# Layer 3's causal mask moves from TensorE to VectorE, with other orders of the attentions' first products

## The chip, the cores and the metric

The kernel runs on one core of a Trainium2 chip. The metric is the device time of one execution in microseconds, the median of several runs. A core has five engines with queues of their own: PE (TensorE, matrix products into PSUM), DVE (VectorE), ACT (ScalarE), POOL (GpSimd) and SP (SyncE). PEld is PE's weight load, which overlaps its products. PSUM has eight banks of 512 fp32 columns; a tile that is computed there holds its banks until its readers are done.

## The reference

The program is a chain of four layers on an input of shape (8, 512, 128), each with half a feed-forward block, a mixer and another half block. The change concerns the mixers of layers 1 and 3, both attentions with 16 heads of 8 dimensions over 512 positions; layer 3's is causal:

```python
def _L3_attn_ref(embeddings, Wq, bq, Wk, bk, Wv, bv, Wo, bo):
    ...
    scores = jnp.einsum('bhqk,bhsk->bhqs', q, k) / jnp.sqrt(jnp.float32(dk))
    causal_mask = jnp.triu(jnp.ones((s, s), dtype=bool), k=1)
    scores = jnp.where(causal_mask, jnp.float32(-1000000000.0), scores)
    weights = jax.nn.softmax(scores, axis=-1)
    ctx = jnp.einsum('bhqs,bhsk->bhqk', weights, v)
    concat = ctx.transpose(0, 2, 1, 3).reshape(b, s, d)
    return concat @ Wo + bo
```

Layer 1's is the same without the mask, with another residual and a normalisation behind it.

## The kernel before

An attention handles one of eight batches after another. The 16 heads are four groups `g` of four heads (`j` or `h`), each head in a band of 32 partitions; the 512 positions are four chunks `c` of 128. The softmax needs each query's largest score before the exponential, with queries on partitions, but the exponentials themselves are made with keys on partitions, so the scores are computed twice:

- The *first products* (`maxima`, PSUM tile `first`, three buffers): for each chunk of queries, head and group, one product of `qT` with `kT`, and a read on DVE (L1673) that puts minus the row maximum into `max`. In layer 3 chunk c needs only its first 128 (c + 1) keys. There the diagonal block is masked on PE: a product of a bf16 identity with a bf16 mask tile (0 or -1e30) is added into the same PSUM columns behind the first product. Chunks 1 and 0 are narrow, so two groups' products of chunk 1 (2 x 256 columns) and four groups' products of chunk 0 (4 x 128) share one bank and one read. That makes 64 first products and 44 reads a batch in layer 3, 64 and 64 in layer 1. `firsts` lists their order. When a group's 16 maxima are there, POOL makes `copies`; `maxima_turned` turns all of them by PE into `mT`.
- The *weighted sums* (`weighted`): a step for each group and chunk of keys, in two halves of two heads. A half makes two score products (`pair`, a tile of two banks, two buffers), adds minus the maxima by two more products (`mT`, `max_rows`), and ACT takes the exponential into `e` (L1781). In layer 3 chunk c of keys has only the 512 - 128 c queries from its own on, and POOL clears the upper triangle (L1783). At the end of a second half, `product` multiplies the `e` of the step *before* with `v` and adds into `av`; after the last step of a pair of groups ACT copies `av` to `ctx`.

The first products of batch b + 1 run beside the weighted sums of batch b: each half-step takes two of them from the list. In layer 1 both stand between the half's score products and its max_rows products; in layer 3 both stand behind the max_rows products. Their reads are issued behind the exponential, and a mask product with its read.

PE's order is the order of emission (`in_order`). The other work of a batch (projections of batch b + 2, spreading of q and k over the bands by `spread_out`, the turning of maxima, the end of batch b - 1) is cut into pieces, and `_SLOTS` says behind which of the 32 half-steps each piece stands. `lead` is how many first products of batch 1 run before the first half-step. `fill` is a list by chunk: so many products of a bf16 tile of zeros with one of ones, 512 columns, are added into `av` behind the sums with v of that chunk, which changes no value; layer 3 has (0, 2, 0, 1), layer 1 none.

The 64 first products of batch 0 of layer 3, with their reads, are pieces of `attention_head`; they run among the end of the experts, in tiles that are called `mm` there.

All products go through one helper, so their line is L329 and they are told apart by tiles: `pair<-qkT` scores, `first<-qkT` first products, `first<-mask,ident_bf` masks, `pair<-mT,max_rows` maxima, `av<-e,v` sums, `av<-ones,zeros` fills, `pair<-lead,spread` and `pair<-trail,spread` spreads. L1595 makes the second half of q and k in two parts, and L1338 is a running sum of layer 2.

Of the kernel before, what the change touches and what calls it, by code (L numbers as in the profile page):

```python
# [26 lines left out]
P = 128  # L27
# [175 lines left out]
def _attention_pack(p, wq, bq, wk, bk, wv, bv, wo, bo):  # L203
# [30 lines left out]
        lead=4, attended=(6, 9, 10), spread=(2, 3), turned=30,  # L234
        projected=(3, 5, 5, 7, 12, 18, 19), spread0=(20, 24), fill=(0, 2, 0, 1),
# [56 lines left out]
class _Kernel:  # L292
# [1138 lines left out]
    def attention_constants(self, ctx):  # L1431
# [8 lines left out]
        self.mask = keep.tile([P, 4, P], BF16, name="mask")  # L1440
        self.ident_bf = keep.tile([P, P], BF16, name="ident_bf")
# [25 lines left out]
        nc.vector.tensor_copy(self.mask, self.wide(self.w["const", "mask_qk"]))  # L1467
        nc.vector.tensor_copy(self.ident_bf, self.ident)
# [3 lines left out]
    def attention(self, key, causal):  # L1472
# [9 lines left out]
        with ExitStack() as s:  # L1482
# [6 lines left out]
            for g in range(2 if causal else 1):  # L1489
                self.spread_out(1, g)  # L1490
# [51 lines left out]
    def between(self, b):  # L1542
# [10 lines left out]
        if b + 1 < NB:  # L1553
            late = (2, 3) if self.causal else (1, 2, 3)
            put(at["spread"], [lambda g=g: self.spread_out(b + 1, g) for g in late])
            put([at["turned"]], [lambda: self.maxima_turned(b + 1)])
        if b + 2 < NB:
            put(at["projected"], self.projections(b + 2))
            early = (0, 1) if self.causal else (0,)
            put(at["spread0"], [lambda g=g: self.spread_out(b + 2, g) for g in early])  # L1560
# [82 lines left out]
    def maxima(self, b):  # L1643
# [7 lines left out]
        def product(c, j, gs, k, bank):  # L1651

# [3 lines left out]
            if k == 0:  # L1656
                name, bufs = self.banks["first"]
                bank.append(self.ps.tile([P, L], F32, name=name, bufs=bufs))
            sc = bank[0][:, : len(gs) * n].rearrange("p (g n) -> p g n", n=n)
            self.mm(  # L1660
                sc[:, k, :],
                q["qT"][gs[k]][r, bass.ts(c, P)],
                q["kT"][gs[k]][r, :n],
                start=k == 0,
                stop=not causal,
            )
            if k + 1 < len(gs):
                return None

            def read():  # L1670
                if causal:
                    self.mm(sc[:, :, n - P :], self.ident_bf, self.mask[:, : len(gs), :], start=False)
                nc.vector.tensor_reduce(  # L1673
                    mx[:, c, j, gs[0] : gs[-1] + 1], sc, AX.X, ALU.max, negate=True
                )
# [241 lines left out]
```

## Time and profile before

| what | us |
|---|---|
| median of 3 runs | 2370.53 |
| lowest and highest run | 2366.5, 2375.26 |
| span of the profiled execution | 2372.5 |
| layer 1's attention, about | 803 to 1251 |
| one batch of it | 54.0 |
| layer 3's attention, about | 1900 to 2300 |
| one batch of it | 51.6 |

The profile is one execution. A line of a group gives the kernel's line, engine, operation, output and input tiles and shapes, the count, then busy time and mean length of one, then the idle time of the engine just before such instructions and what ended it. A chain of waits is followed back from the last instruction to what released each one. Products on PE are pipelined, so the length of one holds its latency; the distance from start to start says what it takes of PE. Layer 3's batch holds on PE 32 mask products of 128 columns, 8 of 256 and 4 of 512:

```profile
L329 PE MATMUL first<-mask,ident_bf 128*128 128x128 bf16 x32 | 4.6, 224 | 0.0
L329 PE MATMUL av<-ones,zeros 128*128 128x512 bf16 x12 | 4.0, 384 | 0.0
L329 PE MATMUL first<-mask,ident_bf 128*128 128x256 bf16 x8 | 2.3, 283 | 0.0
L329 PE MATMUL first<-mask,ident_bf 128*128 128x512 bf16 x4 | 1.6, 389 | 0.0
```

### The profile page before, as it was taken

The page shows a single profiled execution, that of the slowest core. Times are in us where ns is not written, and L with a number is a line of the kernel's source. Part 1 is how long each engine was busy: PE and PEld are TensorE (multiplying, and loading weights), DVE is VectorE, ACT ScalarE, POOL GpSimd, SP SyncE. Part 2 cuts the span into 40 slices and gives each one's busy share as a digit, 9 for nine tenths or more (in the row PEclk, how much of TensorE's full clock was granted, in tenths as well). Part 3 has the DMA queues.
Part 4 walks back from the last instruction along what each step waited for, and adds up shares of the span by engine and source line. Part 5 has one row for each costly group of instructions (what it writes and reads, how often), then busy time and mean ns, then how long its engine had stood idle before and what let it go on. Part 6 is the DMA issues. An engine that isn't in the chain of part 4 may idle for free.

```text
span 2372.5 us, 30011 instructions
## 1 busy us (share of the span) xinstructions
PE 2109.1 (89%) x10967; PEld 1001.9 (42%) x10967; DVE 1631.6 (69%) x3830; ACT 1269.6 (54%) x1857; POOL 660.6 (28%) x923
## 2 busy tenths in 40 slices
PE   7679999979998888999996999896789999999989
PEld 3344444444433333333332444444445444444444
DVE  4556775368888788888827889888776556666611
ACT  3545665323322376777772446666674355555554
POOL 1124433013212011111113233446552123333330
PEclk9778998979999999999997999998897999999999
DMA  3000000000000000000000000000000000000001
GB/s 124 1 1 1 1 1 1 14 10 1 1 1 1 1 1 1 1 1 1 1 1 7 1 1 1 0 1 1 0 1 0 1 1 1 1 1 1 2 1 36
DMA packets 10035, 13.07 MB, mean 6 GB/s; under 512 B 416, under 2 KB 8736, under 8 KB 9760
## 3 DMA queue, kind: packets, MB, share of 16 engines
q1 hardware_dynamic: 7776, 10.11, 1.3%
q8 instruction: 86, 1.41, 0.3%
q10 hardware_dynamic: 2112, 1.05, 0.2%
q14 instruction: 61, 0.50, 0.1%
HBM read 9.06 MB, written 2.10 MB: 5 GB/s over the span
## 4 chain that ended last, share of the span: by engine, by line
PE 60%; DVE 23%; POOL 7%; ACT 7%; issue 3%; DMA 0%; ACTq 0%; DVEq 0%; SPq 0%; POOLq 0%
PE pair L329 11%; PE av L329 8%; PE mm L329 8%; PE po L329 6%; PE pu L329 5%; PE first L329 4%; DVE max L1673 4%; PE pg L329 3%; ACT e L1781 3%; PE ck L329 2%; PE pr L329 2%; DVE act L942 2%; PE big L329 1%; PE ph L329 1%; DVE xn L355 1%
## 5 line engine op out<-in xcount | busy, mean ns | idle before, releaser
L1673 DVE TENSOR_REDUCE max<-first 128x1 f32<-128x512 f32 (+3 forms) x756 | 468.3, 664 | 173.4 <-PE first L329 166.1
L1781 ACT ACTIVATE e<-pair 128x1024 f32<-128x1024 f32 (+3 forms) x512 | 436.5, 864 | 239.3 <-PE pair L329 227.1
L329 PE MATMUL first<-qkT 32*128 32x512 f32 (+3 forms) x896 | 267.9, 443 | 30.5 <-DVE max L1673 28.7
L329 PE MATMUL pair<-qkT 32*128 32x512 f32 (+3 forms) x1024 | 222.5, 454 | 20.0 <-ACT e L1781 14.6
L329 PE MATMUL av<-e,v 128*32 128x512 f32 (+3 forms) x2048 | 238.9, 536 | 0.1
L941 ACT ACTIVATE act<-pg 128x512 f32<-128x512 f32 x144 | 85.6, 596 | 212.9 <-PE po L329 122.0
L329 PEld LDWEIGHTS pair<-qkT 32*128 32x128 f32 x1024 | 95.2, 185 | 233.6 <-ACT e L1781 133.2
L329 PE MATMUL pair<-mT,max_rows 32*128 32x512 f32 (+3 forms) x1024 | 190.4, 374 | 1.7 <-DVE mT L1715 1.7
L329 PE MATMUL pu<-xT,w_moe 128*128 128x512 f32 x288 | 158.4, 632 | 18.8 <-DVE act L942 14.0
L1783 POOL TENSOR_SCALAR_AFFINE_SELECT e<-e 128x256 f32<-128x256 f32 x256 | 103.4, 407 | 253.4 <-ACT e L1781 253.1
L329 PE MATMUL po<-act,w_moe 128*128 128x512 f32 x288 | 161.3, 647 | 5.4 <-DVE act L949 4.2
L329 PE MATMUL pg<-xT,w_moe 128*128 128x512 f32 x288 | 150.5, 620 | 4.4 <-ACT act L941 3.3
L329 PEld LDWEIGHTS first<-qkT 32*128 32x128 f32 x896 | 119.6, 185 | 69.4 <-DVE max L1673 66.9
L942 DVE TENSOR_TENSOR act<-act,pu 128x512 f32<-128x512 f32 x144 | 97.8, 679 | 28.8 <-PE pu L329 23.5
L1679 POOL COPY copies<-max 128x128 f32<-128x128 f32 x64 | 23.6, 424 | 272.4 <-DVE max L1673 272.4
L329 PEld LDWEIGHTS pair<-mT,max_rows 32*128 32x128 f32 x1024 | 96.9, 188 | 3.0 <-DVE mT L1715 2.7
L1673 DVE TENSOR_REDUCE max<-mm 128x1 f32<-128x512 f32 (+3 forms) x108 | 70.9, 665 | 36.7 <-PE mm L329 35.5
L949 DVE TENSOR_TENSOR act<-act,big 128x512 f32<-128x512 f32 x128 | 86.3, 677 | 12.3 <-PE big L329 11.8
L329 PEld LDWEIGHTS pu<-xT,w_moe 128*128 128x128 f32 x288 | 50.2, 196 | 76.8 <-DVE act L942 37.0
L329 PEld LDWEIGHTS po<-act,w_moe 128*128 128x128 f32 x288 | 50.5, 199 | 63.5 <-issue 28.1
L978 POOL TENSOR_TENSOR ge<-ge,w_moe 128x64 f32<-128x64 f32 (+1 forms) x32 | 42.8, 1336 | 119.1 <-DVE ge L976 113.6
L329 PEld LDWEIGHTS pg<-xT,w_moe 128*128 128x128 f32 x288 | 51.1, 195 | 57.2 <-issue 40.1
(423 smaller groups left out, 4398.2 us busy)
## 6 DMA issues: line engine op xcount, KB each, us to landing
w_moe<-in_moe SPq DMA_DIRECT2D x1, 2392.0 KB, 14.0
out<-x SPq DMA_DIRECT2D x8, 256.0 KB, 2.3
x<-in_u ACTq DMA_DIRECT2D x4, 256.0 KB, 6.6
x<-in_u SPq DMA_DIRECT2D x4, 256.0 KB, 6.4
w_mixer<-in_l0a SPq DMA_DIRECT2D x1, 960.5 KB, 8.2
w_mixer<-in_l1a SPq DMA_DIRECT2D x1, 769.0 KB, 4.8
w_ffn<-in_l0f SPq DMA_DIRECT2D x1, 578.0 KB, 7.2
w_ffn<-in_l2f SPq DMA_DIRECT2D x1, 560.0 KB, 3.3
```

The lines of the kernel that those rows point to most:

```text
L329: self.nc.tensor.matmul(out, lhsT, rhs, start=start, stop=stop)
L355: nc.vector.tensor_scalar(xn[:, c, :], x[:, c, :], mv[:, c, 0:1], rstd[:, c : c + 1], ALU.subtract, ALU.mult)
L941: nc.scalar.activation(act, pg, AF.Silu)
L942: nc.vector.tensor_tensor(act, act, pu, ALU.mult)
L949: nc.vector.tensor_tensor(act, act, pw[:, e % 2, :], ALU.mult)
L978: nc.gpsimd.tensor_tensor(ge.rearrange(flat), ge.rearrange(flat), self.wide(before, m), ALU.mult)
L1673: nc.vector.tensor_reduce(mx[:, c, j, gs[0] : gs[-1] + 1], sc, AX.X, ALU.max, negate=True)
L1679: nc.gpsimd.tensor_copy(copies[:, :, :, :, g], mx[:, :, :, g].unsqueeze(3).to_broadcast([P, NC, 4, 8]),)
L1781: nc.scalar.activation(e[:, :, :n], sc[:, :, :n], AF.Exp, scale=scale)
L1783: nc.gpsimd.affine_select(e[:, :, :P], e[:, :, :P], pattern=[[0, 2], [1, P]], compare_op=ALU.is_ge, fill=0.0, base=0, channel_multiplier=-1,)
```

## The change

In layer 3 every first product gets a bank and a read of its own, as wide as itself. The mask product goes; the read is one DVE instruction that adds a bf16 mask row to the scores, writes the negated sums to a bf16 tile that nothing reads, and takes their minimum. The mask tile is now 512 columns, zeros but for the last 128, made on POOL. The chunks are taken in the order 1, 0, 3, 2 for each group, and with a lead of 8 the half-steps of chunk 0 of keys take first products of chunk 3, and so on by falling width.

In both layers the first half of a step takes its two first products between its score and its max_rows products; the second half takes one there, and its other one, with its read, behind the sums with v. Layer 3's fills are set to none, its slots are set anew, and only group 0 is spread two batches ahead.

```diff
     "l3a": dict(
-        lead=4, attended=(6, 9, 10), spread=(2, 3), turned=30,
-        projected=(3, 5, 5, 7, 12, 18, 19), spread0=(20, 24), fill=(0, 2, 0, 1),
+        lead=8, attended=(6, 9, 10), spread=(1, 9, 17), turned=29,
+        projected=(3, 5, 5, 7, 12, 18, 19), spread0=(23,), fill=(0, 0, 0, 0),
     ),
...
-        self.mask = keep.tile([P, 4, P], BF16, name="mask")
-        self.ident_bf = keep.tile([P, P], BF16, name="ident_bf")
+        self.mask = keep.tile([P, L], BF16, name="mask")
...
-        nc.vector.tensor_copy(self.mask, self.wide(self.w["const", "mask_qk"]))
-        nc.vector.tensor_copy(self.ident_bf, self.ident)
+        nc.gpsimd.memset(self.mask, 0.0)
+        nc.gpsimd.tensor_copy(self.mask[:, L - P :], self.w["const", "mask_qk"])
...
-            for g in range(2 if causal else 1):
-                self.spread_out(1, g)
+            self.spread_out(1, 0)
...
-            late = (2, 3) if self.causal else (1, 2, 3)
-            put(at["spread"], [lambda g=g: self.spread_out(b + 1, g) for g in late])
+            put(at["spread"], [lambda g=g: self.spread_out(b + 1, g) for g in (1, 2, 3)])
...
-            early = (0, 1) if self.causal else (0,)
-            put(at["spread0"], [lambda g=g: self.spread_out(b + 2, g) for g in early])
+            put(at["spread0"], [lambda: self.spread_out(b + 2, 0)])
...
-        def product(c, j, gs, k, bank):
+        def product(c, j, g):
...
-            if k == 0:
-                name, bufs = self.banks["first"]
-                bank.append(self.ps.tile([P, L], F32, name=name, bufs=bufs))
-            sc = bank[0][:, : len(gs) * n].rearrange("p (g n) -> p g n", n=n)
...
+            name, bufs = self.banks["first"]
+            sc = self.ps.tile([P, L], F32, name=name, bufs=bufs)[:, :n]
+            self.mm(sc, q["qT"][g][r, bass.ts(c, P)], q["kT"][g][r, :n])
...
                 if causal:
-                    self.mm(sc[:, :, n - P :], self.ident_bf, self.mask[:, : len(gs), :], start=False)
-                nc.vector.tensor_reduce(
-                    mx[:, c, j, gs[0] : gs[-1] + 1], sc, AX.X, ALU.max, negate=True
-                )
...
+                    unused = self.early.tile([P, L], BF16, name="unused", bufs=1)
+                    nc.vector.tensor_tensor_reduce(
+                        out=unused[:, :n],
+                        in0=sc,
+                        in1=self.mask[:, L - n :],
+                        scale=-1.0,
+                        scalar=3e38,
+                        op0=ALU.add,
+                        op1=ALU.min,
+                        accum_out=out,
+                    )
+                else:
+                    nc.vector.tensor_reduce(out, sc, AX.X, ALU.max, negate=True)
...
-        out = []
-        for g in range(0, 4, 2):
-            for h in (g, g + 1):
-                out += [(c, j, (h,), 0) for c in (3, 2) for j in (2, 3, 0, 1)]
-            out += [(1, j, (g, g + 1), k) for j in (2, 0, 3, 1) for k in range(2)]
-        for pair in ((2, 0), (3, 1)):
-            out += [(0, j, (0, 1, 2, 3), 2 * k + i) for k in range(2) for j in pair for i in range(2)]
-        return out
+            return [(c, g) for g in range(4) for c in range(NC)]
+        return [(c, k // 4) for k, c in enumerate([1, 0, 3, 2] * 4)]
...
-            if not causal:
-                reads = [first() for first in firsts]
+            reads = [first() for first in firsts[: 2 - pair]]
             for h in heads:
                 r = bass.ts(h, 32)
                 self.mm(sc[:, h % 2, :n], self.max_rows[r, g, :], q["mT"][r, q0:], start=False)
-            if causal:
-                reads = [first() for first in firsts]
...
             if pair == 1:
                 self.product()
                 self.unmultiplied = (q, g, c, es)
+                for first in firsts[len(reads) :]:
+                    first()()
```

## The prediction

> **What bounds the kernel now.** I read the page first, then busy times of single batches, then the instructions in order of time, and last the chain of waits.
>
> ```profile
> span 2372.5 us, 30011 instructions
> PE 2109.1 (89%) x10967; PEld 1001.9 (42%) x10967; DVE 1631.6 (69%) x3830; ACT 1269.6 (54%) x1857; POOL 660.6 (28%) x923
> ```
>
> PE is the fullest engine, but that is a mean over stages. The change touches layer 1's attention (about 803 to 1251 us) and layer 3's (1900 to 2300 us), and the 64 first products of batch 0 that run ahead of layer 3 among the experts. Both attentions repeat one batch eight times, so one batch of each is enough; the columns are the stretch, its length, and the busy time (and count) of PE, PEld, DVE, ACT and POOL, then the granted clock.
>
> ```profile
> core 0: us, PE busy (x) PEld busy (x) DVE busy (x) ACT busy (x) POOL busy (x), PEclk, DMA share, GB/s
> 967.00:1021.00 54.00, 48.85 (x368) 19.98 (x367) 45.86 (x85) 39.66 (x43) 8.69 (x11) 1.00 0.00 1
> 2001.60:2053.20 51.60, 49.82 (x436) 24.20 (x438) 33.14 (x65) 29.80 (x44) 16.56 (x39) 1.00 0.00 1
> ```
>
> Layer 3's batch (second row) is PE's: 49.8 of 51.6 us, while DVE has 18 us to spare. Layer 1's batch has PE at 48.85 and DVE at 45.86 of 54.0: two full engines that hold each other up, which costs 5.15 us over PE's work.
>
> What a mask product costs PE is seen by laying a half-step of layer 3 beside one of layer 1, both 512 wide:
>
> ```profile
> 2022.75 0.50 PE L329 MATMUL pair<-qkT 32*128 32x512 f32 x2
> 2023.09 0.39 PE L329 MATMUL pair<-mT,max_rows 32*128 32x512 f32 x2
> 2023.42 0.28 PE L329 MATMUL first<-mask,ident_bf 128*128 128x256 bf16 x1
> 2023.63 0.49 PE L329 MATMUL pair<-qkT 32*128 32x512 f32 x2
> ```
>
> ```profile
> 981.46 0.50 PE L329 MATMUL pair<-qkT 32*128 32x512 f32 x2
> 981.80 0.39 PE L329 MATMUL pair<-mT,max_rows 32*128 32x512 f32 x1
> 981.80 0.48 PE L329 MATMUL pair<-qkT 32*128 32x512 f32 x2
> ```
>
> With a mask, the next pair starts 0.88 us after this one (2022.75 to 2023.63); without one, 0.34 us (981.46 to 981.80), beside the max_rows products. So a mask in a first half costs 0.54 us: its own 0.21, and the overlap that it breaks. In a second half the sums with v follow anyway: from max_rows to av it is 0.54 us with the mask (2023.96 to 2024.50) and 0.42 without (982.79 to 983.21), so 0.12.
>
> The reads of layer 3's batch on DVE (form, count, busy us, mean ns, idle before):
>
> ```profile
> L1673 DVE TENSOR_REDUCE max<-first 128x1 f32<-128x512 f32 x16 | 10.3, 683 | 3.3 <-PE first L329 3.3
> L1673 DVE TENSOR_REDUCE max<-first 128x1 f32<-128x384 f32 x16 | 8.1, 551 | 2.4 <-PE first L329 2.3
> L1673 DVE TENSOR_REDUCE max<-first 128x2 f32<-128x512 f32 x8 | 5.5, 689 | 4.9 <-PE first L329 4.9
> L1673 DVE TENSOR_REDUCE max<-first 128x4 f32<-128x512 f32 x4 | 2.8, 692 | 6.8 <-PE first L329 6.7
> ```
>
> 44 reads, 26.7 us; DVE's other work is 33.1 - 26.7 = 6.4 us. Each read waits for PE, not PE for it.
>
> Layer 1's chain of waits (start, length, what) over one plain step:
>
> ```profile
> 1021.31 0.43 PE pair L329 x2
> 1021.74 0.09 PE first L329
> 1021.83 0.69 DVE max L1673
> 1022.52 0.04 issue
> 1022.56 0.50 PE first L329
> 1023.06 0.01 PE pair L329 x2
> 1023.07 1.00 PE av L329 x8
> ```
>
> The step's fourth first product needs the bank of its first one (there are three), so PE stands until that read is over, and max_rows and av stand behind it: 2.75 us a step, where DVE's four reads take 2.48 (four in 2.48 at 982.03).
>
> **Part by part, layer 3.** *Masks off PE.* 28 of 32 half-steps end one, 14 of each half: 14 x 0.54 + 14 x 0.12 = 9.2 us a batch. Lower bound, if other waits fill the broken overlap: 28 x 0.12 = 3.4.
>
> *Products of ones with zeros.* Two behind each c = 1, one behind each c = 3. The two at 2019.46 delay the next pair to 2020.00, 0.54 us; 4 x 0.81 = 3.2 us.
>
> *The late first product.* It loses its company: before, it ran beside the pair. A 512-wide product in a row of its kind takes 0.235 us (the spreads start at 2012.79, 2013.10, 2013.34, 2013.57), so over the widths 0.235, 0.18, 0.12, 0.06, sixteen a batch: + 2.4 us. Where it meets PE waiting, nothing.
>
> PE's work in a batch: 49.8 - 9.2 - 3.2 + 2.4 = 39.8 us.
>
> *Reads on DVE.* 64 instead of 44, each as wide as its product. From the rows, 0.644 us (10.3/16) at 512 and 0.506 at 384, so 0.138 per 128 columns: 0.368 and 0.230; 16 of each, 28.0 us. The fused mask-and-minimum has no row here. From below: a tensor_tensor of 512 from PSUM (677 to 679 ns) costs no more than the reduce, so nothing extra. From above: it writes a second output, so I add one smallest DVE instruction (128x1 TENSOR_SCALAR, 145 ns): 64 x 0.145 = 9.3. Nearest is an instruction with three inputs, L1595's scalar_tensor_tensor, 740 against 683 ns, so I take 0.07: 4.5 us. DVE's work: 6.4 + 28.0 + 4.5 = 38.9 us (34.4 to 43.7). A gain below the reduce is excluded, since it reads as many elements and one operand more. [...]
>
> *The batch.* PE 39.8 and DVE 38.9 are now as close as in layer 1, so I add layer 1's 5.15: 45.0. Another way: DVE's four reads set plain steps (2.86, 2.30, 1.76, 1.20 by width, 32.5 for four rounds), and PE's pieces between steps come on top, in layer 1 54.0 - 16 x 2.48 = 14.3: 46.8, less what the spreads moved into slots 1, 9 and 17 hide behind wide reads. I take 46.0, 5.6 less than 51.6; seven batches have first products beside them: **-39.2**. Bounds 43.6 (three spreads of 1.1 hidden) to 51.8 (DVE's 43.7 and the 8.1 that layer 1 has over DVE). The last batch loses only its fills: **-3.2**.
>
> *Slots and lead.* The moved spreads, projections and turns issue the same products on the same queues; no DMA is moved. Two spreads early become one, and turned goes from 30 to 29: nothing, covered by PE's other work, 1.1 us a spread if not. Eight narrow reads in the lead (4 x 0.44 + 4 x 0.30 = 3.0) for four of 512 (4 x 0.62 = 2.5), and four products more (4 x 0.12): **+1**.
>
> *Ahead of layer 3.* 44 reads there take 27.8 us; 64 take 32.5, and 44 masks leave PE. There (1700 to 1900 us) DVE is busy for 131.6 of 200 us and PE for 177.1, so I set +4.7 against -44 x 0.12 = -5.3: **0**, bounds -10 to +10. The mask's two POOL instructions in setup are hidden behind layer 1's experts; about 1 us if not.
>
> *Clock.* In layer 3's steady part it is 1.00, but not always:
>
> ```profile
> 2259.90:2263.90 4.00, 3.42 (x33) 1.44 (x33) 0.75 (x1) 2.85 (x6) 1.11 (x3) 0.96 0.00 0
> 2263.90:2267.90 4.00, 4.00 (x28) 1.10 (x26) 0.00 (x0) 2.22 (x5) 0.92 (x3) 0.50 0.01 4
> ```
>
> A stretch with PE at 3.42 of 4 us is followed by half clock until about 2273.8, so 10 us at half, at most 5.1 us lost. Steps that wait for DVE thin PE out; I set two more such drops: **+10.2** (0 to 71). [...]
>
> **Layer 1.** The wait before the fourth product moves behind av, about 1.4 us later, when the read has long ended. Behind it now stands the next step's pair, and ACT's exponentials behind that. Plain steps go from 2.75 to DVE's 2.48, nine a batch: -2.4. The seven others follow ACT's chain (pair, e, pair, av), and there the lone product adds 0.235: +1.6. Net -0.8, seven batches: **-5.6** (bounds -17 and +11).
>
> **Sum.** -39.2 - 3.2 + 1 + 10.2 - 5.6 = -36.8 from 2372.5 is 2335.7; the profiled execution is 2.0 over the median of 2370.53, so **2334 us**, 1.5% less. Own range 2318 to 2352.
>
> **Rivals.** *Larger gain:* batch 43.6, layer 1 at -17, no drop: -56 - 3 + 1 - 17 = 2296. For it: the spreads sit where DVE is widest. Against: layer 1 never hides so well.
>
> *DVE takes over (slower):* place, the reads of layer 3; price 0.29 us over the reduce, two smallest instructions, each with its gap. DVE's batch is 6.4 + 28.0 + 18.6 = 53.0; with 3 us of waits 56, +4.4 x 7 = 31, half of the head's 18 shows, less 9 elsewhere: 2402. It decides from 0.14 us a read, where 43.5 and layer 1's 8.1 make 51.6. For it: the scan L1338 takes 1305 ns for 512. Against: plain two-input rows stay at 680.
>
> *The clock falls (slower):* place, the wide-read steps, without fills. Two drops a batch, 14 x 5.1 = 71 on 2323.5: 2395. It decides from nine drops. Against: layer 1, with DVE at 85% and no fills, has 1.00 in the same view.
>
> *No change:* the freed PE time becomes waiting for ACT (e waits for pair in 18 places a batch); about 2366. Against: ACT has 29.8 of 51.6.
>
> **How the numbers follow.** Forecast 0.38, larger gain 0.17, no change 0.09, DVE 0.18, clock 0.18. This kernel's measurement tells about 0.5%, 12 us, from no change. Faster 0.55, same 0.10, slower 0.35. The range reaches to the larger gain and to both slower cases, 2290 to 2405, leaving out some 0.17.
>
> **What would show it.** Right: a layer 3 batch of 44 to 48 us, PE near 40 and DVE near 39 in it; no row of mask or zeros; TENSOR_TENSOR reads at 0.70 to 0.75 us for 512; layer 1's batch near 53. Wrong: reads over 0.83 us, PE's clock under 0.95 inside layer 3, or PE first waiting for DVE max more than 5 us a batch.

## The result, and the profile after

The changed kernel takes 2406.6 us (median of five runs, 2401.9 to 2442.2) against 2370.5: a ratio of 1.0148 with a 95% interval of 1.0123 to 1.0174. It is slower by some 35 us; the forecast was 2334. The longest of the five counts as a slow run and does not enter the ratio.

The profiled execution has a span of 2417.3 us, 44.8 over that of before. Its mean granted clock is 0.912, where the three shorter runs have 0.920 to 0.922; from these means it has 425 us at half clock and they 374 to 385 (the records of the clock in the profiles of before and after are 1.0 or 0.5, nothing between), so the stages below hold some 40 to 50 us more of it than those runs. Cut at the turnings of the maxima and at the last copies of `ctx`, the two spans compare so (us; half clock is the time in which the profile shows PE's granted clock at 0.5):

| stage | before | after | half clock before | after |
|---|---|---|---|---|
| ahead of layer 1's attention | 803.2 | 798.8 | 146.8 | 133.1 |
| layer 1's attention | 435.4 | 451.0 | 20.5 | 27.3 |
| between the attentions | 665.1 | 663.1 | 109.2 | 115.9 |
| layer 3's attention | 395.2 | 426.6 | 20.5 | 136.7 |
| behind it | 73.5 | 77.8 | 0.0 | 12.7 |

So the loss is in the two attentions: 15.6 us in layer 1, 31.4 in layer 3.

The page of the changed kernel, its span and its engines' busy times:

```profile
span 2417.3 us, 30238 instructions
PE 2122.1 (88%) x10504; PEld 1013.4 (42%) x10519; DVE 1671.4 (69%) x4500; ACT 1263.1 (52%) x1857; POOL 666.0 (28%) x925
```

PE has 463 products fewer in its records and is still busy for 13 us more: its products take longer or overlap less. The busy times by stretch show both, the second in layer 1. They are, in this order, one batch of layer 1, one of layer 3, then a piece of that batch of layer 3, and last the interval between the last two turnings of layer 3 (the seventh batch's sums, beside which no projections and no early spreads are left); below it is the same interval before. Columns as before: stretch, length, PE, PEld, DVE, ACT, POOL, granted clock, DMA share, GB/s.

```profile
1038.30:1095.50 57.20, 53.09 (x379) 22.16 (x381) 46.86 (x85) 39.55 (x44) 8.70 (x11) 1.00 0.00 1
...
2025.00:2079.70 54.70, 48.35 (x380) 23.86 (x382) 38.17 (x150) 29.42 (x44) 17.02 (x39) 0.91 0.00 1
...
2046.20:2049.60 3.40, 3.05 (x32) 1.41 (x24) 2.48 (x15) 2.00 (x4) 2.05 (x4) 1.00 0.03 7
2049.60:2053.00 3.40, 2.70 (x33) 1.51 (x29) 2.89 (x18) 0.87 (x3) 2.03 (x4) 1.00 0.01 2
2053.00:2063.20 10.20, 10.03 (x40) 4.31 (x39) 4.38 (x13) 5.34 (x7) 1.70 (x5) 0.50 0.00 0
...
2243.80:2302.50 58.70, 54.57 (x355) 26.75 (x354) 33.89 (x135) 26.92 (x39) 16.99 (x39) 0.59 0.01 1
```

```profile
2213.90:2259.60 45.70, 43.90 (x406) 20.83 (x408) 29.58 (x56) 26.10 (x39) 16.53 (x39) 1.00 0.00 1
```

Layer 3's batch went from 51.6 to 54.7 us, and its clock from 1.00 to 0.91. In five batches in a row, at the same place, PE has a thin stretch (here 3.05 and 2.70 of 3.40 us) while DVE works through ten reads and the twelve pieces of a normalisation; then the clock is 0.50 for 10.2 us, and PE is full because its products take longer (10.03 us busy for 40 of them): a spread of 512 columns starts 0.42 to 0.43 us behind the one ahead of it there (2055.69, 2056.12, 2056.54), where the kernel before has 0.23 to 0.24 at clock 1.00 (2013.10, 2013.34, 2013.57). The last interval is worse: clock 0.59, 58.7 us where before had 45.6.

The reads of that batch on DVE, by form:

```profile
L1659 DVE CUSTOM_DVE_ANT_0 unused<-first,mask 128x512 bf16<-128x512 f32 x16 | 11.1, 692 | 3.2 <-PE pair L329 1.1
...
L1659 DVE DVE_READ_ACCUMULATOR2_ANT max<- 128x1 f32 x64 | 5.3, 83 | 0.0
```

Each fused read is two instructions. Their busy times alone look cheap (692 + 83 ns); the order of time shows what a read takes of DVE:

```profile
2028.15 0.69 DVE L1659 CUSTOM_DVE_ANT_0 unused<-first,mask 128x512 bf16<-128x512 f32 x1
2028.77 0.08 DVE L1659 DVE_READ_ACCUMULATOR2_ANT max<- 128x1 f32 x1
2028.99 0.69 DVE L1659 CUSTOM_DVE_ANT_0 unused<-first,mask 128x512 bf16<-128x512 f32 x1
```

Four plain reduces before the change, in one row:

```profile
982.03 2.48 DVE L1673 TENSOR_REDUCE max<-first 128x1 f32<-128x512 f32 x4 [0.37 <-PE pair L329]
```

The fused read takes 0.84 us from start to start. The plain ones take 0.60: 2.48 us from the first start to the last end, less the 0.69 of the last, over three. So it is 0.24 more, not 0.07 (the 0.62 and the 0.21 of some expectations are the same rows with the last one's end counted in).

Layer 1's chain of waits (start, length, what) over one plain step of the changed kernel:

```profile
1044.20 0.70 DVE max L1670
...
1044.95 0.49 PE first L329
...
1045.44 1.00 PE av L329 x8
1046.44 0.43 PE first L329
...
1046.90 0.70 DVE max L1670
```

The wait for a bank did not go, it moved: `av`, then the late product alone (0.43), its read (0.70), then the next first product, for which the read had to make room. The seven plain steps of a batch are 2.70 us instead of 2.75, while seven of the nine others, which follow ACT, became 0.2 to 0.5 us longer (3.57 to 3.8 to 4.0, 4.25 to 4.64 and 4.73). So the batch went from 55.2 to 57.2 us from turning to turning. The 54.0 of the table ahead is the length of a stretch that was cut out, not of a batch.

### The profile page after: what moved, and what is told of

It is laid out like the page before. It is cut to its first block, busy times and chain, and to the rows that moved or that the text cites. A ratio compares the mean times of both kernels' runs of the same rounds, so it can differ in the third digit from the quotient of the medians.

```text
span 2417.3 us, 30238 instructions
## 1 busy us (share of the span) xinstructions
PE 2122.1 (88%) x10504; PEld 1013.4 (42%) x10519; DVE 1671.4 (69%) x4500; ACT 1263.1 (52%) x1857; POOL 666.0 (28%) x925
## 4 chain that ended last, share of the span: by engine, by line
PE 58%; DVE 24%; POOL 7%; ACT 7%; issue 4%; DMA 0%; DVEq 0%; ACTq 0%; SPq 0%; POOLq 0%
PE pair L329 9%; PE av L329 8%; PE mm L329 8%; PE po L329 6%; PE first L329 5%; PE pu L329 5%; PE pg L329 4%; DVE max L1670 3%; DVE unused L1659 3%; ACT e L1764 3%; PE ck L329 2%; PE pr L329 2%; DVE act L942 1%; PE big L329 1%; PE ph L329 1%
## 5 line engine op out<-in xcount | busy, mean ns | idle before, releaser
L329 PE MATMUL first<-qkT 32*128 32x512 f32 (+3 forms) x896 | 296.0, 483 | 36.5 <-DVE max L1659 18.9
L1670 DVE TENSOR_REDUCE max<-first 128x1 f32<-128x512 f32 x448 | 283.0, 684 | 58.9 <-PE first L329 53.5
L1659 DVE CUSTOM_DVE_ANT_0 unused<-first,mask 128x256 bf16<-128x256 f32 (+1 forms) x448 | 219.5, 490 | 113.5 <-PE first L329 64.2
L329 PE MATMUL pair<-qkT 32*128 32x512 f32 (+3 forms) x1024 | 264.4, 451 | 31.9 <-ACT e L1764 12.7
L329 PE MATMUL av<-e,v 128*32 128x512 f32 (+3 forms) x2048 | 250.4, 560 | 0.0
L329 PEld LDWEIGHTS first<-qkT 32*128 32x128 f32 x896 | 125.6, 194 | 259.6 <-DVE max L1670 122.2
L329 PE MATMUL pair<-mT,max_rows 32*128 32x512 f32 (+3 forms) x1024 | 232.3, 419 | 0.8 <-DVE mT L1701 0.8
L329 PEld LDWEIGHTS pair<-qkT 32*128 32x128 f32 x1024 | 123.0, 197 | 119.4 <-ACT e L1764 59.1
L329 PEld LDWEIGHTS pair<-mT,max_rows 32*128 32x128 f32 x1024 | 114.0, 201 | 2.2 <-DVE mT L1701 1.1
L1635 ACT CAST qkT<-pair 128x1024 fp32r<-128x1024 f32 x56 | 56.7, 1013 | 43.5 <-PE pair L329 43.1
L329 PEld LDWEIGHTS po<-act,w_moe 128*128 128x128 f32 x288 | 49.9, 196 | 63.4 <-issue 27.2
```

Of the source, the lines that this page charges most:

```text
L329: self.nc.tensor.matmul(out, lhsT, rhs, start=start, stop=stop)
L1635: self.nc.scalar.copy(t, p)
L1659: nc.vector.tensor_tensor_reduce(out=unused[:, :n], in0=sc, in1=self.mask[:, L - n :], scale=-1.0, scalar=3e38, op0=ALU.add, op1=ALU.min, ...
L1670: nc.vector.tensor_reduce(out, sc, AX.X, ALU.max, negate=True)
```

## The experiments

The theory at the outset: layer 3's PE work did fall, but PE's work became thinner, and the granted clock took the gain back; layer 1's loss is the late product. The rival: DVE, with dearer and more reads, sets layer 3's batch. In the expectations "the last batch" means the interval between the last two turnings (45.6 us before, 58.7 after). "Layer 3" and "half clock" are from each kernel's profiled execution, one each; intervals are from turning to turning, the commonest or the span of the first six. The whole series:

| kernel | us (median) | ratio to before, 95% | layer 3 | half clock in it | interval |
|---|---|---|---|---|---|
| before | 2370.5 | 1 | 395.2 | 20.5 | 51.5 |
| changed | 2406.6 | 1.0123 to 1.0174 | 426.6 | 136.7 | 54.7 |
| changed, layer 1's order back (e1) | 2396.2 | 1.0067 to 1.0138 | 426.7 | 133.3 | 54.7 |
| changed, plain reads (e2) | 2404.7 | 1.0095 to 1.017 | 420.7 | 144.9 | 54.6 |
| changed, old fills (e3) | 2426.6 | 1.02 to 1.0272 | 434.9 | 112.8 | 52.7 to 65.5 |
| before, no masks (e4) | 2365.8 | 0.9954 to 0.9996 | 397.4 | 75.3 | 49.1 to 55.0 |
| before, late product in layer 1 (e5) | 2381.3 | 1.0025 to 1.0067 | 404.0 | 41.0 | 50.8 to 54.6 |
| before, no fills (e6) | 2377.9 | 1.0013 to 1.0074 | 405.6 | 81.9 | 52.7 to 54.4 |
| changed, no late products (e7) | 2427.2 | 1.0179 to 1.0266 | 456.7 | 235.6 | 61.4 |
| e1 with 32 fills a batch (e8) | 2402.3 | 1.0096 to 1.017 | 430.9 | 17.1 | 56.4 |
| e7 with 16 fills (e9) | 2381.1 | 1.0031 to 1.0062 | 411.1 | 27.6 | 54.5 |
| e7 with 32 fills (e10) | 2398.0 | 1.0091 to 1.0133 | 431.3 | 34.4 | 55.4 |
| e1 with 16 fills (e11) | 2429.6 | 1.0215 to 1.0264 | 458.4 | 150.5 | 61.5 |
| e10 with plain reads (e12) | 2389.8 | 1.0055 to 1.0098 | 417.8 | 21.5 | 54.4 |
| before, wide masks on DVE (e13) | 2380.2 | 1.0008 to 1.0052 | 406.1 | 61.4 | 52.1 to 56.5 |
| e13 with more fills (e14) | 2384.3 | 1.0032 to 1.0064 | 409.6 | 41.0 | 52.0 to 56.4 |
| e9 with the old slots (e15) | 2377.8 | 1.0006 to 1.0032 | 405.3 | 51.2 | 51.1 to 56.6 |
| e10 with the old slots (e16) | 2380.3 | 1.0025 to 1.005 | 407.5 | 17.1 | 52.6 |
| e15 with 24 fills (e17) | 2380.1 | 1.0024 to 1.0051 | 406.5 | 37.5 | 51.8, 54.6 |
| changed, old slots (e18) | 2422.8 | 1.0178 to 1.0249 | 434.2 | 187.7 | 53.2 to 57.8 |

In nine of these eighteen (e3, e7, e8, e10, e11, e13, e14, e15 and e18) the kernel took longer than the first of its theories said.

### Layer 1: the late product (e1, e5)

e1 takes the late product out of layer 1 of the changed kernel, e5 puts it into layer 1 of the kernel before. e1's edit:

```diff
-            reads = [first() for first in firsts[: 2 - pair]]
+            reads = [first() for first in (firsts[: 2 - pair] if causal else firsts)]
```

> The changed kernel with layer 1's first products all back in front of max_rows; layer 3 keeps the late one. If the late product is what lengthened layer 1's batch (55.2 us before, 57.2 after), it returns to 55.2 and the whole is 12 to 16 us under the changed kernel, about 2392; layer 3 stays at 54.7 a batch with one drop of the clock in each. If layer 1's loss has another cause (a shifted clock at its start), its batch stays at 57 and the whole within 4 us of 2406.

> The kernel before, with one thing of the change alone: in layer 1 the second half-step's second first product and its read stand behind the sums with v. Layer 3 is untouched. Theory (the late product is a loss in layer 1, since it stands alone on PE between the sums with v and the next pair, and the next step's bank waits for its read): layer 1's attention 435.4 -> about 450 us, its batches 55-57 -> 57-61, the kernel 2370 -> 2382 to 2387. Rival 1 (my prediction's step: the wait before the fourth product goes and nothing takes its place): layer 1 about 430, the kernel 2363 to 2368. Rival 2 (layer 1's loss in the changed kernel comes from elsewhere, code loading or the mask's place in memory): the kernel stays within 3 us of 2370.

Layer 1's attention went from 451.0 to 437.5 us without the late product, and in the kernel before from 435.4 to 448.4 with it: 13.5 and 13.0, both ways. In a batch of e1, PE is busy for 3 us less than in the changed kernel's (53.09), at the same clock:

```profile
1029.20:1084.40 55.20, 50.07 (x376) 20.58 (x376) 46.78 (x86) 40.22 (x44) 8.68 (x11) 1.00 0.00 1
```

This is settled: the late product costs layer 1 about 13 us, 2 a batch, where the prediction had a gain of 5.6. In e5's profile layer 3, which is that of before instruction for instruction, takes 404.0 instead of 395.2 us, with a drop of 6.8 us to half clock in four of its batches. That what comes ahead decides this is not shown: the stage between the attentions has less half clock in that profile (81.9 us for 109.2), and e5's ten runs have 266 to 316 us of it in all, the kernel before 264 to 329.

### The reads on DVE (e2, e12)

Both replace the fused read by a plain reduce of the same width, which leaves the mask of the first products out, e2 in the changed kernel, e12 in e10 (no late products, 32 fills a batch), where half clock in layer 3 is 34.4 us, against 235.6 without the fills:

```diff
-                if causal:
-                    unused = self.early.tile([P, L], BF16, name="unused", bufs=1)
-                    nc.vector.tensor_tensor_reduce(
...
-                else:
-                    nc.vector.tensor_reduce(out, sc, AX.X, ALU.max, negate=True)
+                nc.vector.tensor_reduce(out, sc, AX.X, ALU.max, negate=True)
```

> The changed kernel with layer 3's fused read replaced by the plain reduce of the same width. It leaves out the mask of the first products in layer 3: the number subtracted there is then a maximum over up to 127 later keys too, which the softmax divides out. If the fused read's extra time on DVE (0.85 against 0.62 us from start to start at 512) is what bounds layer 3, its batch falls from 54.7 to 45 to 48 us and the half-clock stretches inside it go, whole 2345 to 2360. If the missing fills are the cause by themselves, the clock still falls once a batch and the batch stays over 51, whole over 2380.

> The run with no late products and two fills a step (2398 us, batches 55.4 at clock 1.00), with each fused read replaced by a plain reduce of the same width; layer 3's mask is left out of the maxima. Theory 1 (with the clock held, DVE's reads set the batch: 64 x 0.21 = 13 us of DVE less): the batch falls by 3 us or more, to 48-52, with the clock still at 1.00, layer 3 from 431 to 395-410, the kernel to 2360-2380. Theory 2 (PE's own work and its waits for ACT's copies and the turned maxima set it): the batch falls by no more than the 2.8 us that PE waits for DVE max there, to 52.6-55.4, the kernel to 2378-2398.

With 64 reads cheaper by 0.24 us each, about 15 us of DVE a batch, the changed kernel stays where it was: intervals of 54.6, half clock 144.9 instead of 136.7. With the clock held, the interval falls from 55.4 to 54.4:

```profile
2060.20:2114.60 54.40, 47.95 (x412) 22.17 (x412) 34.21 (x85) 29.86 (x43) 16.65 (x39) 1.00 0.00 1
```

So the reads cost 1 us a batch at full clock and nothing that shows at the clock of the changed kernel. The rival "DVE takes over" falls, although the read is dearer than its deciding point of 0.14.

### The masks alone (e4, e13, e14)

e4 takes the mask products out of the kernel before and puts nothing in their place, so it leaves that mask out; e13 moves those of chunks 3 and 2 into a fused read that writes back to PSUM, all else as before; e14 adds eight fills a batch.

e4:

```diff
...
-                if causal:
-                    self.mm(sc[:, :, n - P :], self.ident_bf, self.mask[:, : len(gs), :], start=False)
```

e13:

```diff
...
+                if causal and c >= 2:
+                    nc.vector.tensor_tensor_reduce(
+                        out=sc[:, 0, :],
+                        in0=sc[:, 0, :],
+                        in1=self.mask_row[:, L - n :],
...
```

> The kernel before with the mask products taken off PE and nothing put in their place; it leaves out the mask of the first products in layer 3, as the plain reduce does. If the forecast's price of a mask on PE is right (9.2 us a batch), layer 3's batch falls from 51.6 to 43 to 46 us and the whole to 2310 to 2335. If the masks were hidden behind other waits (3.4 us a batch or less), the batch stays over 48 and the whole over 2345.

> The kernel before, with its order, banks, fills and slots, and only the masks of chunks 3 and 2 moved from PE into a fused read on DVE (32 of the 44 reads); the fused read writes its unused output back to PSUM. Theory (masks off PE are worth about 2 us a batch while the clock holds, and the thinner PE brings drops as in the run of before without masks: 75 us of half clock): batches of 49 to 50 without a drop and 54-55 with one, half clock in layer 3 of 30 to 80 us, the kernel 2358 to 2372. Rival 1 (forecast's pricing: 32 of the masks are worth 6 us or more a batch): batches of 46, the kernel under 2340. Rival 2 (the fused reads themselves cost): DVE has 18 us of idle time in this batch and the reads add 32 x 0.21 = 6.7; if they cost all the same, the batches are above 52 without a drop and the kernel above 2375.

> The same with fills (1, 2, 1, 1) for (0, 2, 0, 1), eight products more, 2.2 us of PE's time. Theory: less half clock than in the run with the fills of before (under 40 us), batches 50 to 52.5, the kernel 2355 to 2370: what the fills hold of the clock, they take of PE. Rival: the half clock stays as it is, and the kernel is 15 us slower than the run with the fills of before.

e4 is what the forecast rested on, by itself and free of DVE. Priced at 9.2 us a batch, the masks would bring 64 us over seven batches. They bring 1 to 11 us in all, and layer 3 is not shorter at all (397.4 against 395.2). Its one batch without a drop:

```profile
2053.00:2102.10 49.10, 43.35 (x387) 21.59 (x392) 32.57 (x65) 29.15 (x43) 16.40 (x39) 1.00 0.01 1
```

49.1 us, 2.4 less than before; PE's busy time fell by 6.4 (some 1.9 of that are fills whose records are missing, five of twelve at 0.38), and PE waits longer, 4 to 6 us where it was 1.8. The other intervals are 50.8 to 55.0 with half clock in them. e13 and e14 missed their ranges on the slow side (2358 to 2372 and 2355 to 2370 were expected): a batch without a drop has 52.0 us in e14, not 50, and the others have drops. e13's time is the one that its second rival named (above 2375), but not by that rival's reason: written back to PSUM, the fused read is only 0.02 to 0.05 us dearer than a reduce (rows in the last section), not 0.21. Why these batches are longer than e4's stays open. No version with a mask on DVE gained.

### Fills and the clock (e3, e6, e8 to e11)

The edits are the list `fill` alone: e3 puts (0, 2, 0, 1) back into the changed kernel, e6 sets it to none in the kernel before, e8 gives e1 two behind each step, e11 one. e8's against e1:

```diff
-        projected=(3, 5, 5, 7, 12, 18, 19), spread0=(23,), fill=(0, 0, 0, 0),
+        projected=(3, 5, 5, 7, 12, 18, 19), spread0=(23,), fill=(2, 2, 2, 2),
```

> The changed kernel with layer 3's products of ones with zeros back, (0, 2, 0, 1). If the clock is a cost of its own, the stretch of 10.2 us at half clock in each batch goes and the batch falls to 51 to 52 us, whole about 2385, and the long stretch in the last batch goes too. If DVE is the bound, the fills run in PE's waits, the batch stays within 1.5 us of 54.7 whether the clock falls or not, and only the last batch gains, 5 to 10 us, whole 2396 to 2402.

> The kernel before with layer 3's fills (products of ones with zeros) set to none, nothing else. They take 12 x 0.27 = 3.2 us of a batch. Theory (the fills held the granted clock; without them PE's work is thinner and the clock falls to half for 10.2 us about once a batch): half-clock time in layer 3 goes from 20.5 us to 70 or more, layer 3 from 395 to between 395 and 410, the last batch from 45.6 to 50 or more, the kernel 2368 to 2385. Rival (fills only cost PE's time; the clock falls because of masks and waits alone): half clock in layer 3 stays under 35 us, the batches go from 51.6 to 48.4, the kernel 2345 to 2350.

> The changed kernel with layer 1's order back and fills of two products of ones with zeros behind each step's sums with v in layer 3: 32 a batch, at 0.27 us 8.6 us of PE's time, of which a part falls into waits. Theory (the granted clock falls when PE is thin, and it is the clock that costs the changed kernel its gain): half-clock time in layer 3 falls from 133 us to under 50, the last batch from 58.7 to 46-50 us, the other batches from 54.7 to 50-56 although PE has more to do, layer 3 from 427 to 400-415, the kernel from 2396 to 2370-2385. Rival (half clock is set by something that fills do not reach): half clock stays above 100 us, batches grow to 60 or more, layer 3 to 450 or more, the kernel 2415 or more.

> The changed kernel with layer 1's order back and one fill behind each step's sums with v in layer 3: half of the fills of the run before (2402 us, 17.1 us of half clock, batches 56.4), where none gave 2396 us, 133.3 us and 54.7. Theory (the clock and the fills' cost trade one for the other): half clock between 20 and 100 us, batches 51 to 56, layer 3 405 to 430, the kernel 2375 to 2400: no dose of fills gives the forecast of 46 us a batch. Rival (half of the fills hold the clock at half of the price): half clock under 30 us, batches under 52.5, the kernel under 2375.

e6 gives the sign: without its fills the kernel before does not gain 3.2 us a batch, it loses 7 us in all; half clock in layer 3 goes from 20.5 to 81.9 us, the intervals from 51.5 to 52.7-54.4. Only its last interval (45.2) did not go as expected. e8 shows that products alone can hold the clock: 32 that change no value take the half clock of layer 3 from 133.3 to 17.1 us, and the last interval from 51.9 us to 49.9. But they do not make the kernel faster, 2402 against 2396: the batches are 56.4 us long at clock 1.00.

```profile
2064.40:2120.80 56.40, 49.20 (x406) 23.32 (x414) 38.42 (x149) 29.57 (x44) 16.83 (x39) 1.00 0.00 1
```

Layer 3 was expected at 400 to 415 us and took 430.9, so what the clock gives back, the fills and the waits at full clock take. In this order half a dose is no compromise: e3 and e11 move the drops to other places and are among the slowest, 2427 and 2430, with 112.8 and 150.5 us of half clock. With 16 fills there is more half clock than with none (133.3), so their number alone does not decide.

What half clock costs can be estimated from the runs of one kernel among themselves, since each run has its mean granted clock. The kernel before was run some 95 times beside these experiments: its half clock was 264 to 329 us (median 294), and the time rose by 0.35 us with each us of it. Over the runs of all kernels, each against its own kernel's mean, it is 0.33. So a us of half clock goes with a third of a us; half a us is the most if no product takes more than twice its time there, and the spreads of 512 columns take 1.8 times (0.42 to 0.43 us for 0.23 to 0.24). By this price, an estimate, the changed kernel's usual 374 to 385 us cost it some 30 us more than before, e6's 347 (the median of its runs) some 17, and e4's 341 some 15: at the half clock of before, e4 would have gained some 20 us of the 64.

### No late products (e7, e9, e10)

```diff
-            reads = [first() for first in firsts[: 2 - pair]]
+            reads = [first() for first in firsts]
```

This is e7; e9 and e10 add one and two fills a step.

> The changed kernel with both first products of a second half in their earlier place, between the scores and the max_rows products, in both layers: no late product and no late read. Layer 1 as in the run with layer 1's order back: about 437 us. Theory (the clock takes back in layer 3 what PE's work is less, wherever the first products stand): half-clock time in layer 3 stays above 100 us, layer 3 at 415 to 435, the kernel at 2390 to 2405. Rival (in layer 3 too the late product is what makes PE wait, so without it PE is dense, the clock holds): half clock in layer 3 under 50 us, batches under 50 us, the kernel under 2360.

> The changed kernel without late products in both layers, and one fill (a product of ones with zeros) behind each step's sums with v in layer 3: 16 a batch, 4.3 us of PE's time. Without fills this order had batches of 61.4 us and 235.6 us of half clock in layer 3. Theory (half clock comes from thin PE work; the batch would be about 61.4 - 17 = 44.4 us at full clock): half clock falls to between 60 and 150 us, batches 50 to 57, layer 3 from 457 to 400-435, the kernel from 2427 to 2370-2405. Rival (this order has waits of its own that the clock only follows): batches stay at 60 or more, the kernel 2420 or more.

> The same with two fills behind each step's sums: 32 a batch, 8.6 us of PE's time. Theory: half clock in layer 3 under 50 us, batches about 44.4 + 8.6 = 53 us (51 to 56), layer 3 395 to 420, the kernel 2360 to 2390. Rival (the late product is worth something apart from the clock, as the order with it was 30 us faster without fills): batches of 57 or more at full clock, above the 56.4 of the order with it and the same fills, the kernel above 2402.

Without fills the earlier place of the products makes layer 3 worse, 456.7 us with 235.6 of half clock. With one fill a step it is far better than the order with the late product (2381 against 2430), with two about the same (2398 against 2402). At clock 1.00 the late product costs layer 3 about 1.0 us a batch (56.4 in e8, 55.4 in e10); beyond that its place has no price that would hold over these runs, and they differ in where and how long the clock drops. e7 and e10 were expected to be faster (2390 to 2405 and 2360 to 2390). e10 at clock 1.00 is the cleanest view of the new arithmetic. One of its batches, then two stretches of another one at the place where the changed kernel drops (28 us and on behind the turning):

```profile
2006.70:2062.10 55.40, 47.68 (x405) 22.49 (x412) 38.36 (x149) 29.86 (x43) 17.01 (x39) 1.00 0.00 1
...
2090.30:2093.70 3.40, 2.83 (x25) 1.21 (x27) 2.15 (x11) 1.53 (x3) 0.82 (x2) 1.00 0.02 5
2093.70:2097.10 3.40, 2.69 (x20) 1.44 (x22) 2.46 (x9) 2.86 (x5) 0.82 (x2) 1.00 0.01 2
```

Here PE is as thin as ahead of a drop in the changed kernel (2.70), and no drop follows. Which stretches bring one is not told by PE's busy share, and these runs leave it open. And the batch has 7.7 us without PE work at full clock, some 2 of them for six fills and another product whose records are missing, where the kernel before has 1.8. What it waits for, in a second batch of the same run and then in a batch before the change (form, count, busy and mean, idle before and what ended it):

```profile
L329 PE MATMUL first<-qkT 32*128 32x128 f32 (+3 forms) x66 | 17.4, 398 | 2.8 <-DVE max L1659 2.8
L329 PE MATMUL pair<-qkT 32*128 32x128 f32 (+3 forms) x66 | 11.9, 385 | 2.8 <-DVE mT L1701 1.1 <-ACT qkT L1635 1.0 <-DVE v L1607 0.5
```

```profile
L329 PE MATMUL first<-qkT 32*128 32x512 f32 (+3 forms) x65 | 17.9, 390 | 0.6 <-DVE max L1673 0.5
L329 PE MATMUL pair<-qkT 32*128 32x128 f32 (+3 forms) x66 | 13.4, 406 | 0.5 <-ACT qkT L1639 0.5
```

It waits for banks that the reads of the maxima free (2.8, and with plain reduces in e12 still 2.5), for the turned maxima (1.1) and for the spread copies (1.0, and 1.2 ahead of other products). The last two are the moved pieces.

### The slots (e15 to e18)

e15 and e16 put the spreads, the turning and the two early groups of before back into e9 and e10; e17 is e15 with fills (1, 2, 1, 2); e18 puts them back into the changed kernel alone. e16's edit against e10:

```diff
-        lead=8, attended=(6, 9, 10), spread=(1, 9, 17), turned=29,
-        projected=(3, 5, 5, 7, 12, 18, 19), spread0=(23,), fill=(2, 2, 2, 2),
+        lead=8, attended=(6, 9, 10), spread=(2, 3), turned=30,
+        projected=(3, 5, 5, 7, 12, 18, 19), spread0=(20, 24), fill=(2, 2, 2, 2),
...
-            self.spread_out(1, 0)
+            for g in range(2 if causal else 1):
+                self.spread_out(1, g)
...
```

> The run with no late products and one fill a step (2381 us, batches 54.6, PE's waits for ACT qkT 2.6 and for DVE mT 1.1 us a batch), with the slots and the two groups spread early as before the change (spread 2 and 3, turned 30, spread0 20 and 24). Theory 1 (the new slots cost PE 2 to 4 us of waits a batch): PE's waits for qkT and mT fall under 1.5 us, the batch to 51-52.5 unless the clock falls, the kernel to 2355-2370. Theory 2 (the slots are nothing, as the prediction had it; the batch follows from PE's work and the reads): the batch stays within 1 us of 54.6, the kernel within 8 us of 2381.

> The same with two fills a step (2398 us and batches of 55.4 at clock 1.00 with the new slots). Theory 1: batches of 52 to 53.5 at clock 1.00, the kernel 2370 to 2385. Theory 2: batches of 55 to 56, the kernel 2392 to 2402.

> The run with no late products and the slots of before, with fills (1, 2, 1, 2), 24 a batch, between the 16 (2378 us; 51.1 us a batch without a drop, half clock of 51.2 in layer 3) and the 32 (2380 us; 52.6, 17.1). Theory (fills and clock trade one for the other, so the changed arithmetic ends within 0.5% of before at best): batches of 51.5 to 52.3 without a drop, half clock of 15 to 50 us, the kernel 2366 to 2380. Rival (at some dose the clock holds at half the price): all batches under 52, half clock under 20 us, the kernel under 2364.

> The changed kernel as it stands (late products, no fills), with the slots and the early spreads of before alone. Theory 1 (the slots' 2.8 us a batch is PE waiting; without fills the clock takes it back, as it did with the masks and the reads): half clock in layer 3 stays at 100 us or more, batches of 53 to 57, the kernel 2395 to 2415. Theory 2 (the waits of the new slots are what makes PE thin and starts the drop of each batch): half clock under 60 us, batches under 52, the kernel under 2385.

At clock 1.00 the old slots take e10's batch from 55.4 to 52.6 us, the commonest interval of e16. One of its batches, and in it the products that waited for the turned maxima, and the fills:

```profile
2159.80:2212.60 52.80, 48.90 (x412) 22.57 (x413) 38.47 (x151) 29.88 (x44) 16.76 (x40) 1.00 0.01 1
```

```profile
L329 PE MATMUL pair<-qkT 32*128 32x128 f32 (+3 forms) x66 | 12.3, 389 | 1.0 <-ACT qkT L1638 0.7 <-ACT e L1767 0.2
L329 PE MATMUL av<-ones,zeros 128*128 128x512 bf16 x32 | 9.7, 385 | 0.0
```

Waits ahead of `pair` fell from 2.8 to 1.0, and the one for the turned maxima is gone from the row. So the new slots cost 2.8 us a batch at full clock. e15's batches without a drop are 51.2, 0.3 less than before the change, but three have drops, and the kernel ends at 2377.8. e17 did not find a dose that holds the clock more cheaply (2380). And e18 gives the counterpart: without fills, the better slots bring nothing, half clock 187.7 us and 2423; the clock takes what they save and more. No kernel here that computes the mask beats the one before; e15 comes nearest, 0.06 to 0.32% over it. The new order of the chunks, the lead of 8 and the banks of their own (64 reads for 44) were not tested by themselves.

## Why the prediction was wrong

*PE's work: forecast 2 to 3 us too small.* 39.8 us a batch were forecast, of which 2.4 for the late products. e16 has none, so its forecast is 37.4; its batch, with all 32 fills in its records, has 48.90 - 9.7 (32 fills of 0.30) = 39.2, or 40.3 with a fill at the prediction's 0.27. The masks were priced too high: 9.2 us, where PE in e4 is busy for some 4.5 us less (6.4 less 1.9).

*DVE's work: forecast too small, right only as busy time.* 38.9 forecast, 38.2 measured as busy, and this agreement is luck, since a gap of 0.14 us follows the accumulator's read (2028.85 to 2028.99). From start to start the fused reads take 0.84, 0.71, 0.58 and 0.44 us by width, 41 us for 64, with the 6.4 of other work some 48, above my bound of 43.7. The fused read takes 0.24 us more than a reduce, not 0.07, and the bounds were 0 to 0.145. The 0.07 came from the length of a single instruction (L1595); the trace shows the fused read as two, of 0.69 and 0.08 us, with that gap behind them. It cost little: 1 us a batch where the clock holds.

*The step that failed: the clock.* "Steps that wait for DVE thin PE out; I set two more such drops: +10.2". The length of one drop was right (10.2 us at half), the number was not: half clock in layer 3 went from 20.5 to 136.7 us, 116.2 more, at most 58 us of time and some 38 at the price of a third, where the sum had 10.2. There was one drop in each batch, and more in the last interval. The rival "the clock falls" (2395) named this mechanism and was given 0.18; its place, the steps with wide reads, was not the place: the drop follows ten reads of 128 to 384 columns that stand beside DVE's normalisation. What spoke against it, layer 1's clean clock at PE 48.85 of 54.0, did not carry over. In the changed kernel the steady drops follow 3.4-us stretches with PE busy for 2.6 to 2.8 of them. But e10 has such a stretch (2.69 of 3.40) without a drop, so it is not shown what starts one; that a stretch in which PE is thin brings a drop was my estimate, from the one drop shown from the profile of before (PE at 3.42 of 4 us).

*The fills: the wrong sign.* "The last batch loses only its fills: -3.2", and 3.2 in each other batch. By e6 they were worth more than they cost: without them the kernel before is 7 us slower.

*The slots: mis-sized.* "...nothing, covered by PE's other work, 1.1 us a spread if not." It was not covered: 2.8 us a batch at full clock (e10 to e16).

*The batch: 46.0.* No run without fills held the clock (81.9 us of half clock or more in layer 3), so its length at full clock was not measured. 54.7 less at most half of 10.2 is 49.6 or more, and 51.3 at the price of a third. From e16 to e15 16 fills less make 52.6 to 51.2, so another 16 would give 49.8, but without late products and with the old slots, which are worth 1.0 and 2.8 us. So 3.6 us of the forecast's 5.6 or more were missing before the clock came in: PE's work was larger than the sum had it, and its freed time turns into waits. e4, free of DVE's new work, saves 2.4 us a batch and not the masks' 9.2.

*Layer 1: the wrong sign.* "The wait before the fourth product moves behind av, about 1.4 us later, when the read has long ended." The read that matters is the late one's own, behind which the next bank comes free. Plain steps became 2.70 us, not 2.48, and they are seven a batch, not nine; with that count the prediction's own prices give no gain. Forecast -5.6, measured +15.6 in the profiled execution, 13 of them by the late product alone.

*The sum.* Layer 3 without the clock's term was forecast at -41.4 us and came out at +31.4, 73 us apart: some 38 of them by the clock (at most 58), the other 35 (at least 15) by work and waits that the sum did not have. Layer 1 adds 21. The stages around them moved by -4.4, -2.0 and +4.3 us, as expected about nothing. Of the three signs of being wrong two came, 0.84 us a read and a clock of 0.91; PE's first products wait for DVE's maxima 2.6 us a batch, not 5.

## What to carry to other kernels

Work that "costs" PE time may be what keeps its clock up (in e6, without 12 fills a batch, half clock in layer 3 went from 20.5 to 81.9 us): before taking products away, look for where the granted clock already drops, and do not count freed PE time as a gain until a run shows it. Measure the removed part alone first (here the masks, without any replacement): it showed in one run that the expected gain of some 64 us was not there. A wait that is moved behind another instruction is followed to the buffer it guards, since the next user of that buffer still waits for it (in layer 1 for a read of 0.70 us).

## What the runs showed of the hardware

- In the profiles of before and after, half-clock stretches come in multiples of 3.4 us (3.4, 6.8, 10.2, 13.7, 20.5 and others, up to 37.5; only the one that the end of each profile breaks off is not), and in the changed kernel's layer 3 a stretch of 10.2 recurs five times, every 54.6 us, 16 such units: the batch keeps step with them, five intervals in a row at 54.7. That many kernels here have intervals of 54.4 to 54.7 us, whatever was changed in them, is seen in the table; that the locking is the reason is not shown.
- The half clock of one and the same code differs from execution to execution: the kernel before has 264 to 329 us of it, and up to layer 1's attention, where before, e4, e5 and e6 are the same, their profiles have 140 to 147 us. A single profile is not enough to say that an edit moved it by a few us.
- The fused read is cheaper where its unused output goes back, as fp32, to the PSUM columns it read: from start to start 0.62 to 0.65 us at 512 columns and 0.48 to 0.52 at 384, against 0.84 and 0.71 with the output in SBUF as bf16, and 0.60 and 0.47 of a plain reduce. Whether the place or the type does it is not shown. In e14, at each width:

```profile
1977.14 0.73 DVE L1674 CUSTOM_DVE_ANT_0 first<-first,mask 128x512 f32<-128x512 f32 x1
1977.79 0.14 DVE L1674 DVE_READ_ACCUMULATOR2_ANT max<- 128x1 f32 x1
1977.79 0.73 DVE L1674 CUSTOM_DVE_ANT_0 first<-first,mask 128x512 f32<-128x512 f32 x1
...
1979.95 0.60 DVE L1674 CUSTOM_DVE_ANT_0 first<-first,mask 128x384 f32<-128x384 f32 x1
1980.46 0.14 DVE L1674 DVE_READ_ACCUMULATOR2_ANT max<- 128x1 f32 x1
1980.46 0.60 DVE L1674 CUSTOM_DVE_ANT_0 first<-first,mask 128x384 f32<-128x384 f32 x1
```

The accumulator's read is longer here than in the changed kernel (0.14 us for 0.08), but the next read starts together with it.
